# Reordering pairs of VO, weight sums and one residual in the first groups of a gated cross-attention block

## The chip, the cores and the metric

The kernel runs on one core of a Trainium2 chip. The metric is the device time of one execution in microseconds, as the median of several runs. The core has five engines that run side by side, each through its own queue of instructions in order: TensorE (PE in the profile; PEld is its loading of weights), VectorE (DVE), ScalarE (ACT), GpSimd (POOL) and SyncE (SP, which issues most DMAs). They wait for one another by semaphores.

## The reference: what is computed

Four sequences of 2048 rows of 512 features attend to a context of 77 keys with 16 heads of 64, and then go through one linear layer that is chosen from eight; both results are added to x through a gate.

```
x = x + tanh(g_xattn[0]) * xattn(layernorm(x), ctx_768, Wq, Wk, Wv, Wo, bo)
x = x + tanh(g_ffn[0])   * ffn(layernorm(x), W, b, logits, u)

xattn: q = x @ Wq ; k = ctx @ Wk ; v = ctx @ Wv           (16 heads of 64)
       attn = softmax(q k^T / 8) ; out = (attn v) @ Wo + bo
ffn:   idx = argmax(log_softmax(logits) + gumbel(u)) ; out = x @ W[idx] + b[idx]
```

All of it is float32.

## The kernel before, in words

**Folded weights.** The kernel doesn't form q, k and v for all rows. It folds Wq and the keys into one matrix M for each head (`build_m`), and the values and Wo into one matrix VO for each head (`build_vo`, L323). Scores of a group of rows are then x·M, and the attention's output is softmax·VO. VO is made in eight pairs of heads: `build_vo(p, engines)` issues six matmuls (three chunks of rows for each of the two heads, of 64 contracted rows) into six PSUM banks, and six evictions that scale by the gate and go to a staging buffer. The string says which engine evicts: its letters are gone through in turn, "A" is ScalarE (L337), "D" is VectorE (L335). Then four DMAs on SP's queue (L341, L342) store the pair in DRAM (`vo_d`). `load_vo(b)` (L348) loads the part that belongs to sequence b back from DRAM as four blocks into `vo`. There are seven staging buffers; five of them lie in `vo` itself, and go round among heads 2 to 15.

**Groups.** 16 groups of 512 rows are worked on, four to a sequence. Of each group come the scores (`ps_s`), the softmax, the attention's output (`ps_a`), the residual, and the feed-forward (`ps_f`). While group i's softmax runs, TensorE does the attention of group j = i - 1 and then its feed-forward.

**Seven products.** Every large product is done with seven products of half size in place of eight (`Seven`, L441). This needs sums of blocks: four of the weights (`weight_sum`, L119, by GpSimd unless told otherwise) and four of the columns, T1 to T4 (`Columns.sum`, L430, GpSimd). A Seven accumulates in three PSUM regions; `product(s)` (L455) is the matmuls of step s, and `post(s)` (L478) then either copies a region to SBUF on ScalarE (L468, L472: the quarters 11, 22, 12 and last 21), or adds it to a quarter on VectorE (L487). So a later product that accumulates into a region waits for the copy or the addition that reads it: products 2, 4 and 6 of a Seven write the region that post(0), post(2) and post(4) have read. Seven PSUM banks serve all products in turn.

**Softmax of one group.** `s_rows` (L513) transposes scores into rows; `head_max` (L523) takes a quarter's maxima, four quarters ("heads" 0 to 3) to a group; `exps(i, n0, n1)` (L529) issues exponentials n0 to n1 of 64 on ScalarE, 16 to a head; `head_sum` (L538) sums and inverts on VectorE; `head_scale` (L543) scales on GpSimd; `p_columns` (L547) transposes back into `pT` on VectorE, and needs all four heads for each piece.

**Residual.** `residual(j, at, which)` (L556) adds a quarter of the attention's output to x on GpSimd. T1 of the feed-forward's columns (`yc`) is the difference of quarters 12 and 11, so it stands behind the residuals in GpSimd's queue.

**What sets the order.** The order is written out by hand: the order of the calls in the program is the order of each engine's queue. The stretch that the change touches is the start. Ahead of the loop over groups stand pairs 0 to 2 of VO, the scores of group 0, pair 3 (L739, "AAD"), then a loop of six products of group 1's scores (L743) with one pair of VO behind each of the first four products (L755: "DDA", "DDA", "D", "D"), the maxima and exponentials of group 0, and the weight sums of wf (the feed-forward's weight) among them. `e` (L742) says how many exponentials are issued by each step; the rest follow the loop (L764). `load_vo(0)` stands in step 3 (L760). The next loop (L765) does the rest of group 1's scores (`s1`, `s2`, and the last product of `s0`), takes group 0's `p_columns` in steps 1 to 4, and the first three weight sums of vo in steps 3, 4 and 5. Group 1's pass through the loop over groups (i = 1, j = 0) then begins with the attention of group 0 (L866), in whose step 0 the fourth sums of vo and of wf are made (L885, L886); in step 5 come a head's sum, its scaling and the residual of quarter 22 (L906 to L908).

Of the kernel before, what the change touches and what calls it, by code (L numbers as in the profile page):

```python
# [19 lines left out]
def flamingo_block_kernel(  # L20
# [34 lines left out]
    NT, D = x.shape  # L55
# [467 lines left out]
    def head_max(i, h):  # L523
        mx = stat[:, ds((16 + h) * NG, NG)]
        nc.vector.tensor_reduce(mx, head(i, h), AX.X, ALU.max)  # L525
        nmx[h] = small.tile([P, NG], F32, tag=f"nmx{h}", name="nmx")
        nc.vector.tensor_tensor(nmx[h], mx, norms[i].down, ALU.mult)  # L527
# [10 lines left out]
    def head_sum(i, h):  # L538
        sums[h] = sm = small.tile([P, NG], F32, tag=f"sm{h}", name="sm")
        nc.vector.tensor_reduce(sm, head(i, h), AX.X, ALU.add)  # L540
        nc.vector.reciprocal(sm, sm)  # L541
# [195 lines left out]
    s2 = Seven("ps_s", w_scores, xc[1], (4,), SNAP1)  # L737
    head_max(0, 0)
    build_vo(3, "AAD")  # L739
    head_max(0, 1)  # L740
    exps(0, 0, 8)
    e = (8, 16, 24, 32, 41, 50, 57)  # L742
    for s in range(6):  # L743
        s0.product(s)
        s0.post(s)
        if s < 2:
            centre_wf(wfr, 2 * s)
            centre_wf(wfr, 2 * s + 1)
        if s == 2:
            weight_sum(wf, 0)  # L750
            weight_sum(wf, 1)
        if s == 3:
            weight_sum(wf, 2)
        if s < 4:
            build_vo(4 + s, "DDA" if s < 2 else "D")  # L755
        if s < 2:
            head_max(0, 2 + s)
        exps(0, e[s], e[s + 1])
        if s == 3:
            load_vo(0)  # L760
        if 3 <= s:
            head_sum(0, s - 3)
            head_scale(0, s - 3)
    exps(0, 57, 64)  # L764
    for s in range(7):  # L765
        s1.product(s)
        s2.product(s)
        if s == 0:
            s1.post(0)
            s2.post(0)  # L770
            s0.product(6)
            s0.post(6)
            head_sum(0, 3)
            head_scale(0, 3)
        if s == 3:
            norm_step(n1, 2)
        if 1 <= s < 5:
            p_columns(0, (0, 2, 5, 7)[s - 1], (2, 5, 7, 10)[s - 1])
        if s == 2:
            pT[0].sum("T1")  # L780
        if s == 3:
            weight_sum(vo, 0)
        if s == 4:
            weight_sum(vo, 1)
        if s == 5:
            weight_sum(vo, 2)
            for k in range(4):
                s_rows(1, (0, 1, KH, KH + 1)[k], s0.chunk(k // 2, k % 2))
        if 0 < s:
            s1.post(s)  # L790
            s2.post(s)
# [5 lines left out]
    for i in range(1, NGRP):  # L797
        j, f, nx = i - 1, i - 2, i + 1
        n = norms[i]
        last = nx == NGRP  # L800
        swap_m, swap_vo = i % GPB == GPB - 1 and not last, 1 < i and j % GPB == 0
        if 1 < i:

            s0 = scores0(i)
            for s in range(6):
                s0.product(s)
                if s == 0:
                    s0.post(0)
                    if 0 <= f:
                        end_of_ff(f)  # L810
                    p_columns(j, 6, 8)
                    xc[i].sum("T4")
                if s == 1:
                    p_columns(j, 8, 10)
                    if 0 <= f:
                        f_rows(f, ff, 1)
                if s == 2:
                    pT[j].sum("T1")
                    pT[j].sum("T3")
                if 0 < s:  # L820
                    s0.post(s)
                if 0 <= f and s in (2, 3):
                    n.stats(ys[f], 0, 8 * (s - 2), 8)
                if s == 3 and 0 <= f:
                    add_bias(f, nc.gpsimd)
            n.gather()
            for k in range(2):
                s_rows(i, k, s0.chunk(0, k))

            s1 = Seven("ps_s", w_scores, xc[i], (2, 3), SNAP)  # L830
            s2 = Seven("ps_s", w_scores, xc[i], (4,), SNAP1)
            for s in range(7):
                s1.product(s)
                s2.product(s)
                if s == 0:
                    s1.post(0)
                    s2.post(0)
                    s0.product(6)
                    s0.post(6)
                    n.calc()  # L840
                    n.power()
                    for k in range(2):
                        s_rows(i, KH + k, s0.chunk(1, k))
                elif s == 3:
                    n.back()
                if swap_vo and 3 <= s:
                    weight_sum(vo, s - 3, nc.vector if s < 5 else None)
                if 5 <= s and 0 <= f:
                    f_scale(f, n.rs, 5 * (s - 5), 5)
                if 0 < s:  # L850
                    s1.post(s)
                    s2.post(s)
                if s == 5:
                    for k in range(2):
                        s_rows(i, 2 + k, s1.chunk(0, k))
                    s_rows(i, 4, s2.chunk(0, 0))
            for k in range(2):
                s_rows(i, KH + 2 + k, s1.chunk(1, k))
            s_rows(i, KH + 4, s2.chunk(1, 0))
            if swap_m:  # L860
                load_m(nx // GPB)
        if not last:
            norms[nx] = Norms(nx)


        at = Seven("ps_a", w_attend, pT[j], (0, 1), SNAP, bo_c)  # L866
        for s in range(7):
            at.product(s)
            if s == 0:
                pT[j].sum("T2")  # L870
                if 0 <= f:
                    f_scale(f, n.rs, 10, 6)
                    f_add(f, 0, NG, nc.gpsimd)
                    store(f)
                head_max(i, 0)
                head_max(i, 1)
            if s == 1:
                head_max(i, 2)
                head_max(i, 3)
            if 1 <= s:  # L880
                e = (0, 10, 20, 32, 44, 56, 64)
                exps(i, e[s - 1], e[s])
            if s == 0 and i == 1:
                pT[j].sum("T3")
                weight_sum(vo, 3)  # L885
                weight_sum(wf, 3)  # L886
            if s == 2:
                pT[j].sum("T4")
                if swap_m:
                    weight_sum(m, 0)  # L890
                if not last:
                    x_columns(nx)
                    norms[nx].stats(xg[nx], norms[nx].x0, 0, 8)
                head_sum(i, 0)
                head_scale(i, 0)
            if s == 3:
                if not last:
                    norms[nx].stats(xg[nx], norms[nx].x0, 8, 8)
                    if nx + 1 < NGRP:
                        load(nx + 1)  # L900
            if s == 4:
                residual(j, at, "11")
                head_sum(i, 1)
                head_scale(i, 1)
            if s == 5:
                head_sum(i, 2)  # L906
                head_scale(i, 2)
                residual(j, at, "22")  # L908
            if s == 6:
                residual(j, at, "12")  # L910
                residual_last(j, at)
                head_sum(i, 3)
            else:
                at.post(s)
        if j % GPB == GPB - 1:
            load_vo((j + 1) // GPB)
        yc[j] = Columns(xc[j].all, **{f"T{k + 1}": tq[:, k] for k in range(4)})
        yc[j].sum("T1")
        yc[j].sum("T2")
        yc[j].sum("T3")  # L920
        head_scale(i, 3)
        yc[j].sum("T4")


        ff = Seven("ps_f", w_ffn, yc[j], (0, 1), SNAP)
        for s in range(6):
            ff.product(s)
            if s < 2:
                y_rows(j, 2 * s)
            if s == 1 and swap_m:  # L930
                weight_sum(m, 1, nc.vector)
            if not last:
                if s == 1:
                    xc[nx].sum("T1")
                if s == 2:
                    xc[nx].sum("T2")
                if s == 4:
                    if swap_m:
                        weight_sum(m, 2)
                    xc[nx].sum("T3")  # L940
                    if swap_m:
                        weight_sum(m, 3)
            if 2 <= s:
                k = (0, 2, 3, 5, 6)
                p_columns(i, k[s - 2], k[s - 1])
            ff.post(s)
        f_rows(j, ff, 0)


    j, f = NGRP - 1, NGRP - 2  # L950
# [146 lines left out]
```

## Time and profile before

| what | us |
|---|---|
| median of 3 runs | 1249.91 (1249.31 to 1250.05) |
| the profiled execution's own time | 1249.17 |
| its span (first to last instruction) | 1247.1 |
| TensorE busy | 1234.9 (99%) |
| TensorE weight loads busy | 1061.0 (85%) |
| VectorE busy | 908.8 (73%) |
| GpSimd busy | 894.8 (72%) |
| ScalarE busy | 683.6 (55%) |

The span is shorter than the execution's time by what lies before the first and behind the last instruction. All times inside the execution are counted from the first instruction. "Busy" is a share of the whole span; the start, where VO is made, has other limits than the fourteen like passes that follow, so the stretch from 88 to 170 us has to be read by itself, engine by engine. A row in order of time gives the start, the length, the engine, the line, the operation, what it writes and reads, how many instructions are merged in it, and in brackets the idle time before it with what ended that. Where an operation has to wait, the bracket names the engine and tile that it waited for; a matmul's wait shows at its weight load.

### The profile page before, as it was taken

What the parts mean: (1) busy time and instruction counts of PE and PEld (TensorE: products, weight loads), DVE (VectorE), ACT (ScalarE), POOL (GpSimd) and SP (SyncE); (2) the same over time, 40 slices, a digit from 0 to 9 for tenths busy, and PEclk for the clock granted to TensorE, in tenths of its full rate; (3) what the DMA queues carried; (4) which work ended last, traced back from release to release, by engine and by line L of the source; (5) the groups of instructions that cost most, each with busy time, mean ns of one, the idle gap of its engine ahead of it and who ended that gap; (6) DMA issues with size and microseconds to landing.
All of it is one profiled execution on the core that took longest, in us unless ns stands there. A gap on an engine that the chain in (4) does not pass through costs nothing.

```text
span 1247.1 us, 16992 instructions
## 1 busy us (share of the span) xinstructions
PE 1234.9 (99%) x5704; PEld 1061.0 (85%) x5704; DVE 908.8 (73%) x1853; ACT 683.6 (55%) x1957; POOL 894.8 (72%) x484
## 2 busy tenths in 40 slices
PE   9999999999999999999999999999999999999996
PEld 6676888888888888888888888888888888888885
DVE  6778966666977766677776767777776787766577
ACT  4639545638274563827356482745648274554823
POOL 5558885857957785785968778575977877575766
PEclk9999999999999999999999999999999999999999
DMA  9868300314023030304006030202305120010102
GB/s 266 309 194 271 60 1 1 68 43 110 1 51 102 1 68 1 68 22 117 15 1 152 1 68 2 55 14 85 68 1 118 35 62 7 1 34 1 34 1 67
DMA packets 95221, 80.27 MB, mean 64 GB/s; under 512 B 3856, under 2 KB 83088, under 8 KB 95136
## 3 DMA queue, kind: packets, MB, share of 16 engines
q1 hardware_dynamic: 92768, 76.74, 24.2%
q10 hardware_dynamic: 1760, 1.34, 0.4%
q0 software_dynamic: 608, 1.13, 0.2%
q8 instruction: 45, 0.74, 0.2%
q14 instruction: 40, 0.33, 0.1%
HBM read 44.07 MB, written 35.13 MB: 64 GB/s over the span
## 4 chain that ended last, share of the span: by engine, by line
PE 94%; DVE 2%; ACT 1%; DMA 1%; POOL 0%; issue 0%; SPq 0%; DVEq 0%; ACTq 0%; POOLq 0%
PE ps_s L462 37%; PE ps_a L462 36%; PE ps_f L462 15%; PE ps_kv L266 2%; PE ps_vo L332 2%; PE ps_m L296 1%; ACT s L533 1%; DVE s L516 0%; DMA vo<-vo_d 0%; DVE pT L553 0%; PE ps_w L167 0%; DVE t L413 0%; DMA vo_d<-vo 0%; DVE snap L487 0%; POOL xc L559 0%
## 5 line engine op out<-in xcount | busy, mean ns | idle before, releaser
L462 PE MATMUL ps_a<-pT,vo 128*128 128x256 f32 x2240 | 486.2, 379 | 0.0
L462 PEld LDWEIGHTS ps_a<-pT,vo 128*128 128x128 f32 x2240 | 425.6, 190 | 57.9
L533 ACT ACTIVATE s<-s,nmx,up 128x77 f32<-128x77 f32 x1024 | 355.6, 446 | 0.9 <-DVE nmx L527 0.8
L433 POOL TENSOR_TENSOR pT<-pT 128x1280 f32<-128x1280 f32 x64 | 185.8, 2904 | 171.6 <-PE ps_a L462 162.0
L462 PE MATMUL ps_s<-tq,m 128*128 128x256 f32 x1280 | 290.6, 380 | 0.0
L462 PEld LDWEIGHTS ps_s<-tq,m 128*128 128x128 f32 x1280 | 242.6, 190 | 36.2 <-issue 1.6
L468 ACT COPY snap<-ps_s 128x512 f32<-128x512 f32 (+1 forms) x188 | 93.5, 515 | 293.4 <-DVE t L413 131.4
L462 PE MATMUL ps_s<-xc,m 128*128 128x256 f32 x960 | 221.0, 379 | 0.0
L462 PEld LDWEIGHTS ps_s<-xc,m 128*128 128x128 f32 x960 | 182.2, 190 | 27.5 <-DVE vo L335 1.6
L544 POOL TENSOR_TENSOR s<-s,sm 128x1232 f32<-128x1232 f32 x64 | 145.1, 2268 | 48.4 <-DVE sm L541 48.4
L487 DVE TENSOR_TENSOR snap<-snap,ps_s 128x512 f32<-128x512 f32 (+1 forms) x141 | 83.7, 593 | 130.4 <-PE ps_s L462 126.3
L462 PE MATMUL ps_f<-tq,wf 128*128 128x256 f32 x512 | 118.5, 379 | 0.5 <-DVE snap L487 0.4
L553 DVE STREAM_TRANSPOSE pT<-s 128x512 f32<-128x512 f32 x160 | 101.0, 678 | 16.8 <-POOL s L544 16.8
L433 POOL TENSOR_TENSOR tq<-xc,tq 128x512 f32<-128x512 f32 x64 | 85.2, 1332 | 35.1 <-PE ps_f L462 32.6
L394 POOL TENSOR_TENSOR r<-r,neghalf 32x16 f32<-32x16 f32 (+1 forms) x33 | 93.1, 2832 | 22.6 <-DVE r L389 22.0
L462 PEld LDWEIGHTS ps_f<-tq,wf 128*128 128x128 f32 x512 | 97.1, 190 | 14.4 <-issue 0.7
L540 DVE TENSOR_REDUCE sm<-s 128x16 f32<-128x1232 f32 x64 | 91.5, 1430 | 20.7 <-ACT s L533 20.6
L516 DVE STREAM_TRANSPOSE s<-snap 128x512 f32<-128x512 f32 x156 | 99.9, 685 | 6.1 <-ACT snap L468 3.9
L525 DVE TENSOR_REDUCE ps_st<-s 128x16 f32<-128x1232 f32 x64 | 92.4, 1444 | 2.1
L462 PE MATMUL ps_f<-xc,wf 128*128 128x256 f32 x384 | 90.7, 379 | 0.0
L433 POOL TENSOR_TENSOR tq<-xc 128x512 f32<-128x512 f32 x64 | 81.4, 1271 | 6.4 <-DVE xc L408 5.1
L468 ACT COPY snap<-ps_f 128x512 f32<-128x512 f32 x63 | 36.9, 585 | 88.9 <-PE ps_f L462 86.2
(129 smaller groups left out, 1186.1 us busy)
## 6 DMA issues: line engine op xcount, KB each, us to landing
xg<-in_x_dram SPq DMA_DIRECT2D x64, 256.0 KB, 5.9
out_dram<-y SPq DMA_DIRECT2D x60, 256.0 KB, 4.8
vo<-vo_d SPq DMA_DIRECT2D x16, 640.0 KB, 5.6
m<-m_d SPq DMA_DIRECT2D x12, 640.0 KB, 4.1
vo_d<-vo SPq DMA_DIRECT2D x14, 512.0 KB, 3.7
m_d<-vo SPq DMA_DIRECT2D x4, 960.0 KB, 6.1
wq<-in_WqT_dram SPq DMA_DIRECT2D x8, 256.0 KB, 7.0
wq<-in_Wo_dram SPq DMA_DIRECT2D x1, 2048.0 KB, 13.2
```

The costliest lines, as they stand in the source:

```text
L266: nc.tensor.matmul(ps[:, :n], w[:, c, ts(p, P)], keys[:, c].rearrange("p b j -> p (b j)"), start=(c == 0), stop=(c == NCC - 1))
L394: nc.gpsimd.tensor_tensor(r, r, neghalf[:32, : r.shape[1]], ALU.pow)
L433: (engine or nc.gpsimd).tensor_tensor(self.at[name], self.at[a], self.at[b_], op)
L462: nc.tensor.matmul(self.ps[r][:, n, :], self.w(blk, c, pair), self.cols(cname, c), start=(first and n == 0 and c == 0), stop=(c == h - 1), ...
L468: nc.scalar.copy(dst, self.ps[r])
L487: nc.vector.tensor_tensor(c, c, self.ps[r], ALU.add)
L516: nc.vector.transpose(key_chunk(sc[i], k), cols.rearrange("p (g h r) -> p g h r", h=HA, r=R))
L525: nc.vector.tensor_reduce(mx, head(i, h), AX.X, ALU.max)
L533: nc.scalar.activation(head(i, h)[:, g, :], head(i, h)[:, g, :], AF.Exp, scale=norms[i].up[:, g : g + 1], bias=nmx[h][:, g : g + 1])
L540: nc.vector.tensor_reduce(sm, head(i, h), AX.X, ALU.add)
L544: nc.gpsimd.tensor_tensor(head(i, h), head(i, h), sums[h].unsqueeze(2).to_broadcast([P, NG, J]), ALU.mult)
L553: nc.vector.transpose(pT[i].all[:, k, :].rearrange("p (g h r) -> p g h r", h=HA, r=R), key_chunk(sc[i], k))
```

## The change

Six edits, all in the start and in the pass i = 1:

- Pair 4 of VO is built directly behind pair 3, ahead of the loop over group 1's products, with its evictions alternating ("AD"). Pairs 5, 6 and 7 move one step forward in the loop; the strings stay with the step and not with the pair.
- The cuts `e` between the exponentials of group 0 are others.
- `load_vo(0)` moves from step 3 to step 2.
- The fourth weight sum of wf moves from the attention of group 0 to step 3 of the loop over group 1's first products.
- The first weight sum of vo moves from step 3 to step 1 of the next loop, ahead of T1 of `pT`.
- In the pass i = 1 the residual of quarter 22 stands ahead of the third head's scaling on GpSimd. In all later passes it stays behind it.

No operation is added or taken away; three evictions go from VectorE to ScalarE.

```diff
     head_max(0, 0)
     build_vo(3, "AAD")
+    build_vo(4, "AD")
     head_max(0, 1)
     exps(0, 0, 8)
-    e = (8, 16, 24, 32, 41, 50, 57)
+    e = (8, 16, 24, 36, 42, 47, 52)
     for s in range(6):
         s0.product(s)
         s0.post(s)
...
         if s == 3:
             weight_sum(wf, 2)
-        if s < 4:
-            build_vo(4 + s, "DDA" if s < 2 else "D")
+            weight_sum(wf, 3)
+        if s < 3:
+            build_vo(5 + s, "DDA" if s < 2 else "D")
         if s < 2:
             head_max(0, 2 + s)
         exps(0, e[s], e[s + 1])
-        if s == 3:
+        if s == 2:
             load_vo(0)
         if 3 <= s:
             head_sum(0, s - 3)
             head_scale(0, s - 3)
-    exps(0, 57, 64)
+    exps(0, 52, 64)
     for s in range(7):
         s1.product(s)
         s2.product(s)
...
+        if s == 1:
+            weight_sum(vo, 0)
         if s == 2:
             pT[0].sum("T1")
-        if s == 3:
-            weight_sum(vo, 0)
         if s == 4:
             weight_sum(vo, 1)
...
             if s == 0 and i == 1:
                 pT[j].sum("T3")
                 weight_sum(vo, 3)
-                weight_sum(wf, 3)
...
             if s == 5:
                 head_sum(i, 2)
+                if i == 1:
+                    residual(j, at, "22")
                 head_scale(i, 2)
-                residual(j, at, "22")
+                if 1 < i:
+                    residual(j, at, "22")
```

## The prediction

> **What bounds the kernel now.** I read the page first, then the list of who waited for whom on TensorE, then each engine's instructions in order of time from 88 to 170 us, the only stretch that the change touches.
>
> ```profile
> PE 1234.9 (99%) x5704; PEld 1061.0 (85%) x5704; DVE 908.8 (73%) x1853; ACT 683.6 (55%) x1957; POOL 894.8 (72%) x484
> ...
> PE 94%; DVE 2%; ACT 1%; DMA 1%; POOL 0%; issue 0%; SPq 0%; DVEq 0%; ACTq 0%; POOLq 0%
> ```
>
> TensorE is the bound. Its matmuls of 128x256 start every 0.216 us from 125 us to the end of the loop, whatever the other engines do; the 16 us after its last matmul (1231.1 to 1247.1) are not touched. So only two things count: matmul time that goes away, and moments at which a matmul is kept waiting. Of the latter the trace has one in this stretch (below: TensorE's weight loads in order of time, the last column being the idle time before and who ended it).
>
> ```profile
> 165.46 1.70 PEld L462 LDWEIGHTS ps_f<-xc,wf 128*128 128x128 f32 x8
> 167.65 0.94 PEld L462 LDWEIGHTS ps_f<-tq,wf 128*128 128x128 f32 x5 [0.49 <-POOL tq L433]
> ```
>
> The matmul before it starts at 167.18, so this one was due at 167.40 and comes at 167.65: 0.25 us lost, and the next follows after 0.32 in place of 0.216: 0.10 more. It waited for GpSimd's T1 of group 0's feed-forward.
>
> **What is nearly late now.** Each engine's rows in order of time: start, length, engine, line, operation, out<-in, number, idle time before and its releaser. Three rows are of ScalarE (ACT), one of GpSimd (POOL), three of VectorE (DVE):
>
> ```profile
> 90.70 2.55 ACT L337 ACTIVATE vo<-ps_vo,tg 128x512 f32<-128x512 f32 x4 [0.68 <-PE ps_vo L332]
> 93.26 1.28 ACT L533 ACT_TABLE_LOAD   x1
> ...
> 106.48 13.83 ACT L533 ACTIVATE s<-s,nmx,up 128x77 f32<-128x77 f32 x40
> ```
> ```profile
> 116.03 8.94 POOL L544 TENSOR_TENSOR s<-s,sm 128x1232 f32<-128x1232 f32 x4 [4.10 <-DVE sm L541]
> ```
> ```profile
> 120.34 1.44 DVE L540 TENSOR_REDUCE sm<-s 128x16 f32<-128x1232 f32 x1
> ...
> 125.01 4.27 DVE L553 STREAM_TRANSPOSE pT<-s 128x512 f32<-128x512 f32 x7 [2.94 <-POOL s L544]
> ...
> 131.91 0.65 DVE L487 TENSOR_TENSOR sn<-sn,ps_s 128x512 f32<-128x512 f32 x1
> ```
>
> Between 90.70 and 121.5 us ScalarE has no idle time before any instruction above 0.02 us. Its last exponential of group 0 ends at 120.30; VectorE starts the last head's sum 0.04 later, ends the reciprocal at 122.06; GpSimd, busy with the third head, starts the fourth scaling at 122.70 (0.6 us of slack) and ends at 124.97; VectorE transposes at 125.01 and is then without a gap until 146 us. In that stretch its addition of 131.91 ends at 132.56; product 6 of s1 accumulates into the bank that it reads, and loads its weights at 132.65. That is 0.09 us of slack on TensorE.
>
> **The change, part by part.**
>
> 1. *TensorE order.* One block of four score matmuls fewer stands between runs of VO. Blocks behind VO take 1.92 us (92.46 to 94.38) where four matmuls take 4 x 0.432 = 1.73: one return trip less is worth 0.19 us. A pair of VO costs 2.92 either way: the run of three pairs starts them at 49.47, 52.29, 55.22 and ends at 58.14. The Trainium skill's page "TensorEngine Tiling (Array Packing)", section "Tiling Modes", has a rule behind this: a change of tiling mode drains TensorE. By that rule alone the change is a gain; it gives no time.
>
> 2. *Evictions on ScalarE.* The fifth pair (build_vo(4)) had "DDA" (two of six on ScalarE) and has "AD" (three); the sixth keeps DDA; the seventh goes from D to DDA; the eighth stays D. So ScalarE gets 8 + 3 = 11 evictions, VectorE 22 - 3 = 19. The three new ones stand ahead of the table load and of all 64 exponentials. The first run of three pairs shows when they can run: its second pair starts at 52.29 and ScalarE's evictions at
>
> ```profile
> 53.45 0.69 ACT L337 ACTIVATE vo<-ps_vo,tg 128x512 f32<-128x512 f32 x1 [0.38 <-PE ps_vo L332]
> 54.31 0.69 ACT L337 ACTIVATE vo<-ps_vo,tg 128x512 f32<-128x512 f32 x1 [0.17 <-PE ps_vo L332]
> 55.32 0.68 ACT L337 ACTIVATE vo<-ps_vo,tg 64x512 f32<-64x512 f32 x1 [0.32 <-PE ps_vo L332]
> ```
>
> that is 1.16, 2.02 and 3.03 after the pair's start. Here the pair starts at 92.46, so the last eviction runs from 95.49 to 96.17, and the table load starts 0.02 later at 96.19, not 93.26: **ScalarE is 2.93 us late**. Behind it everything is back to back and the number of evictions in the loop is the same (2 + 2), so the last exponential ends at 120.30 + 2.93 = 123.23. The lower end is three evictions without waits, 3 x 0.57 (90.70, 91.28, 91.85) = 1.7; the upper end is in rival B. I take 2.93, the row of the same operation.
>
> 3. *The new cuts of the exponentials* (24, 36, 42, 47, 52). On ScalarE nothing stands between the old cuts behind s = 2, nor between the new ones: the built order of ScalarE differs by the three evictions alone. Nothing, either way.
>
> 4. *VectorE gains 3 x 0.66 (95.55, 96.21) = 2.0 us* before 114 us; the first head's sum starts 1.5 earlier (112.7). It doesn't help: the third and fourth sums wait for exponentials 48 (117.4) and 64 (123.23). Fourth: 123.26 + 1.72 (120.34 to 122.06) = 124.98; GpSimd after 0.13, 2.27 long: 127.38; transposes at 127.42. **VectorE is 2.41 late from there**, and has no gap in which to catch up.
>
> 5. *What TensorE feels.* First, s1's product 2 accumulates into what ScalarE copies after the last exponential (120.19 before, 123.12 now, 0.59 long): due at 122.31, it starts at 123.77. Secondly product 6 of s1: addition ends 132.56 + 2.41 = 134.97, and as at 167.59 to 167.65 the matmul follows 0.06 later: 135.03, against 132.86 before: 2.17, and 0.10 for the restart: 2.27. This contains the first, and swallows the 0.19 of part 1.
>
> 6. *Residual "22" ahead of the scaling* (group 1 alone). Addition 22 is done at 157.9; GpSimd idles 2.72 us before the scaling of 161.52, so the residual (1.26) is free there. The chain to T1 is later by 2.41 (exponentials of group 1 start behind VectorE's maxima, 141.65 + 2.41) and shorter by 1.26: T1 ends at 167.59 + 1.15 = 168.74. The weight load is due at 167.18 + 2.27 = 169.45. So the wait at 167.65 goes: -0.25 - 0.10. Without the residual's move T1 would end at 170.0 and cost 0.6.
>
> 7. *Weight sums.* wf 3 (1.26) goes from 149.00, where GpSimd is busy, to 111.94; GpSimd is idle from there to 116.03 (head sum now 114.4). vo 0 (2.91) goes ahead of pT's T1: it starts at 127.4, after its blocks (landed at 122.13 and 124.56 before; the stores end some 2 us earlier now, as does the load behind them on SP's queue), and ends at 130.3; T1 needs five transposes, 130.5, so it costs nothing. vo 1, vo 2, T2 end at 136.9, 139.8, 142.7; they are needed at 141.9, 146.2, 146.2. The skill's "GPSIMD Engine Reference", section "Specifications", speaks against such overlap: GpSimd's way to SBUF contends with some VectorE instructions. The rows disagree for those here: transposes take 0.67 us with GpSimd idle (126.2) and busy (131.3), a 128x1280 sum 2.91 beside them. If it bit, the 3.5 us to T2's deadline would take it.
>
> **Sum**, against the profiled execution (1249.17 us; span 1247.1 and 2.07 around it): +2.27 - 0.35 = **+1.9**, 1251.1. The profiled one lies 0.74 under the median of the three runs, so on the median: 1249.91 + 1.9 = **1251.8 us**. From the lower end of part 2 (1.7: VectorE 1.2 late) it is +0.7.
>
> **Rivals.**
> - *B, slower by more.* Twelve VO matmuls in a row on seven PSUM banks: VectorE reduces head 0's maximum until 92.51 and frees its banks of pair 3 at 93.18 and 93.82. Going round the seven banks in the order in which they come free, only matmul 4 (due 1.39 behind the pair's start, 93.85) needs one. If an earlier one does, the pair stands still: at worst all six behind 93.82, 1.4 us later, and ScalarE with them: +3.3, 1253.2. It decides from 0.6 us of such waiting on. For it: the built order puts a VectorE wait inside this pair. Against: that matmul is the fourth.
> - *C, hidden.* If group 0's exponentials end no later than some 0.7 us after now, only 0.19 and 0.35 are left: 1249.4; partly hidden, up to 1250.9. For it: ScalarE is busy 55% of the span. Against: not in this stretch.
> - *D, it gains what it moves:* faster by 2.5 us or more. TensorE has no such idle time here.
>
> **How the numbers follow.** 0.2% is 2.5 us, about what a measurement of this kernel can tell from no change. Forecast (1250.9 to 1252.4) 0.63; B 0.20; C 0.15; D 0.02. Faster 0.02; within 0.2% 0.63 + 0.15 = 0.78; slower 0.20. The range runs from inside C to inside B, 1249.8 to 1253.0, which leaves about 2 in 10 out.
>
> **What would show it.** In the profile after: the table load at 96.2; the 64th exponential's end near 123.2; the seven transposes at 127.4; weight loads of ps_s that wait for ScalarE's copy near 123.7 and for VectorE's addition near 135; no wait for tq near 169. If the table load stands at 96 and the transposes still start at 125, steps 4 and 5 are wrong; if product 6 isn't kept, the 0.09 us of slack was misread.

## The result and the profile after

| kernel | median us (lowest to highest) | runs | ratio to the kernel before (95% interval) |
|---|---|---|---|
| before | 1249.56 (1248.51 to 1250.09) | 20 | |
| changed | 1251.54 (1250.59 to 1252.10) | 20 | 1.0017 (1.0011 to 1.0023) |

The changed kernel is 2.0 us slower, by its interval 1.4 to 2.9. The forecast was 1.9, and on the median 1251.8. The profiled execution of the changed kernel took 1252.0 us, its span is 1249.8. First the page:

```profile
PE 1235.7 (99%) x5704; PEld 1061.5 (85%) x5704; DVE 907.2 (73%) x1850; ACT 685.4 (55%) x1960; POOL 895.1 (72%) x484
...
PE 96%; DVE 2%; ACT 1%; POOL 0%; issue 0%; DVEq 0%; POOLq 0%
```

The page hides the case: TensorE is busy 0.8 us more, ScalarE has three instructions more and VectorE three fewer, and the shares are as before. What changed is in the list of who waited for whom on TensorE, here the changed kernel's with all its rows:

```profile
PE ps_w L167 <- DVE tq L163: 1.5, 1, 1.5
PE ps_s L462 <- ACT sn L468: 1.3, 1, 1.3
PE ps_s L462 <- DVE sn L487: 0.7, 1, 0.7
PE ps_f L462 <- DVE snap L487: 0.4, 1, 0.4
```

The first and last were there before (the last is in the tail, at 1234.85 before and 1237.53 now). The two in the middle are new: products 2 and 6 of s1. Short waits are not in this list: the one for T1 at 167.65, which the prediction reads from the weight loads, is missing in that of before. ScalarE in order of time shows where they begin:

```profile
91.47 2.55 ACT L337 ACTIVATE vo<-ps_vo,tg 128x512 f32<-128x512 f32 x4 [0.68 <-PE ps_vo L332]
94.39 0.69 ACT L337 ACTIVATE vo<-ps_vo,tg 128x512 f32<-128x512 f32 x1 [0.38 <-PE ps_vo L332]
95.25 0.69 ACT L337 ACTIVATE vo<-ps_vo,tg 128x512 f32<-128x512 f32 x1 [0.17 <-PE ps_vo L332]
96.25 0.68 ACT L337 ACTIVATE vo<-ps_vo,tg 64x512 f32<-64x512 f32 x1 [0.32 <-PE ps_vo L332]
96.95 1.28 ACT L533 ACT_TABLE_LOAD   x1
...
110.17 13.82 ACT L533 ACTIVATE s<-s,nmx,up 128x77 f32<-128x77 f32 x40
```

Here one correction has to be made before any time is compared. In this execution the first matmul of pair 3 starts at 90.31 us, in that of before at 89.54:

```profile
90.31 5.92 PE L332 MATMUL ps_vo<-wq 64*128 64x512 f32 x24
```

(A pair's six matmuls stand as twelve in the profile, so x24 is two pairs.) Up to there the two programs are the same, so the 0.77 us between are an accident of the execution (over all the kernels below the place varied between 88.8 and 92.8). From here on every time "after pair 3" is counted from that matmul. The table load is 6.65 after pair 3, before 3.72: 2.92 late; the copy of s1 (the row that follows the exponentials) 33.58, before 30.65. From the start of pair 3's first matmul to the start of the kernel's last matmul it takes 1148.81 us, before 1146.90: **1.91 us more**. The same measure serves for all the experiments. It is read from the one profiled execution of each kernel. How far it can be trusted shows behind the products with T1 and T2 of group 0's feed-forward: from the matmul that follows them all ten programs are the same, and from there to the last matmul the ten traces differ by up to 0.08 us.

The new waits, in the weight loads in order of time, and what they wait for on VectorE:

```profile
124.51 2.46 PEld L462 LDWEIGHTS ps_s<-tq,m 128*128 128x128 f32 x12 [1.72 <-ACT sn L468]
...
135.79 2.46 PEld L462 LDWEIGHTS ps_s<-tq,m 128*128 128x128 f32 x12 [1.06 <-DVE sn L487]
...
170.22 1.92 PEld L462 LDWEIGHTS ps_f<-tq,wf 128*128 128x128 f32 x9
```
```profile
124.03 1.44 DVE L540 TENSOR_REDUCE sm<-s 128x16 f32<-128x1232 f32 x1 [3.75 <-ACT s L533]
...
128.19 4.27 DVE L553 STREAM_TRANSPOSE pT<-s 128x512 f32<-128x512 f32 x7 [2.44 <-POOL s L544]
...
135.09 0.65 DVE L487 TENSOR_TENSOR sn<-sn,ps_s 128x512 f32<-128x512 f32 x1
```

VectorE sits idle for 3.75 us until the 64th exponential is done. The seven transposes start at 128.19, less 0.77 of the offset 127.42. The addition ends at 135.74, and product 6's weight load starts 0.05 later. At 170.22 the T1 of the feed-forward is no longer waited for. The first matmul of group 0's attention then starts here, in the kernel before and in the changed one:

```profile
135.45 30.38 PE L462 MATMUL ps_a<-pT,vo 128*128 128x256 f32 x140
```
```profile
138.49 30.38 PE L462 MATMUL ps_a<-pT,vo 128*128 128x256 f32 x140
```

That is 45.91 and 48.18 after pair 3: 2.27 later, which T1's missing wait brings down to 1.91 (the matmul behind the products with T1 and T2 starts 81.67 and 83.58 after pair 3).

### The profile page after: what moved, and what is told of

The parts are those of the page before. It is cut to its first block, busy times and chain, and to the rows that moved or that the text cites. A ratio compares the mean times of both kernels' runs of the same rounds, so it can differ in the third digit from the quotient of the medians.

```text
span 1249.8 us, 16992 instructions
## 1 busy us (share of the span) xinstructions
PE 1235.7 (99%) x5704; PEld 1061.5 (85%) x5704; DVE 907.2 (73%) x1850; ACT 685.4 (55%) x1960; POOL 895.1 (72%) x484
## 4 chain that ended last, share of the span: by engine, by line
PE 96%; DVE 2%; ACT 1%; POOL 0%; issue 0%; DVEq 0%; POOLq 0%
PE ps_a L462 39%; PE ps_s L462 37%; PE ps_f L462 15%; PE ps_kv L266 2%; PE ps_vo L332 2%; PE ps_m L296 1%; ACT s L533 1%; DVE pT L553 0%; PE ps_w L167 0%; DVE t L413 0%; DVE snap L487 0%; POOL s L544 0%; DVE t L1018 0%; DVE y L1022 0%; DVE sm L540 0%
## 5 line engine op out<-in xcount | busy, mean ns | idle before, releaser
L544 POOL TENSOR_TENSOR s<-s,sm 128x1232 f32<-128x1232 f32 x64 | 145.2, 2270 | 49.6 <-DVE sm L541 49.6
```

Source lines behind the costliest of these rows:

```text
L544: nc.gpsimd.tensor_tensor(head(i, h), head(i, h), sums[h].unsqueeze(2).to_broadcast([P, NG, J]), ALU.mult)
```

## Experiments

The theory: ScalarE's lateness of 2.9 us behind pair 3, whatever makes it, goes through the exponentials, the last head's sum and scaling, VectorE's transposes and the addition of s1 to TensorE's product 6. The rivals: TensorE's own order, the banks and stores of the run of two pairs cost; or GpSimd's new order does. Each kernel had 11 timed runs beside 33 of the kernel before (one set of 33 for e1 to e4, another for the rest).

| kernel | median us (before) | ratio (95% interval) | pair 3 to last matmul, us | against before |
|---|---|---|---|---|
| before | | | 1146.90 | |
| changed | | 1.0017 (1.0011 to 1.0023) | 1148.81 | +1.91 |
| e1 | 1250.98 (1249.05) | 1.0015 (1.0006 to 1.0024) | 1148.65 | +1.75 |
| e2 | 1251.17 (1249.05) | 1.0018 (1.0009 to 1.0027) | 1148.90 | +2.00 |
| e3 | 1251.78 (1249.05) | 1.0020 (1.0011 to 1.0029) | 1149.32 | +2.42 |
| e4 | 1251.99 (1249.05) | 1.0021 (1.0012 to 1.0030) | 1149.41 | +2.51 |
| e5 | 1249.26 (1249.43) | 0.9997 (0.9988 to 1.0006) | 1146.59 | -0.31 |
| e7 | 1251.18 (1249.43) | 1.0016 (1.0007 to 1.0025) | 1148.81 | +1.91 |
| e8 | 1248.66 (1249.43) | 0.9996 (0.9987 to 1.0005) | 1146.43 | -0.47 |
| e10 | 1251.47 (1249.43) | 1.0017 (1.0008 to 1.0026) | 1148.83 | +1.93 |

**e4: lateness alone, put into the kernel before.**

```diff
     build_vo(3, "AAD")
+    for _ in range(14):
+        nc.scalar.copy(ez, z)
```

> The kernel before with fourteen copies of a 128x8 tile on ScalarE between pair 3's evictions and the table load (some 2.9 us of work that nothing uses); no instruction of any other engine is moved. Theory: the lateness alone makes the loss: VectorE's transposes start 2.4 us later against the table load's old place, product 6 of s1 waits for the addition, and as the residual isn't moved T1 is late too: +2.3 for product 6, +0.5 at T1 in place of the 0.35 of before, together +2.4 us. Rival (the loss needs the reordered TensorE or SP queue): below +0.7 us.

Measured: +2.51. The fourteen copies on ScalarE:

```profile
93.03 3.15 ACT L741 COPY ez<-z 128x8 f32<-128x8 f32 x14
96.19 1.28 ACT L533 ACT_TABLE_LOAD   x1
```

and TensorE's list:

```profile
PE ps_vo L332 <- ACT vo L337: 1.2, 1, 1.2
PE ps_s L462 <- DVE sn L487: 0.4, 1, 0.4
...
PE ps_f L462 <- POOL tq L433: 0.2, 1, 0.2
```

With the kernel before's own order on the other engines, 3.05 us of lateness (6.77 after pair 3 for 3.72) make the whole loss; the row to set beside it is e3 (+2.42, below), which hasn't the residual's move either. How it is split differs: TensorE stands still earlier, at VO matmuls whose banks ScalarE frees late (1.2 us), in place of product 2. That wait is swallowed: product 6 comes when the addition lets it, whatever was lost ahead of it. The rival that needs the reordered queues falls, as a need. That it could be a second cause was not excluded, as the next run showed.

**e1: pair 4's three evictions taken off ScalarE. The expectation failed.**

```diff
-    build_vo(4, "AD")
+    build_vo(4, "D")
```

> The changed kernel with one string changed: pair 4's six evictions all go to VectorE (D for AD), so ScalarE has its old eight evictions and the rest of the change stands. Theory (the cost is ScalarE's lateness of 2.9 us): the gap between the last eviction of pair 3 and the table load on ScalarE is 0.02 us again, the 64th exponential ends 27.0 us after the table load's start as in the kernel before, no weight load of ps_s waits for ScalarE's copy or for VectorE's addition, and the time is 0.5 us UNDER the kernel before (0.19 for the missing return trip, 0.35 for the T1 wait). Rival (the run of two pairs itself costs: banks, staging buffers, stores): 1.5 to 2 us above the kernel before, with waits of TensorE inside the run.

Measured: +1.75, as if nothing had been removed. The table load is back at its place (3.73 after pair 3, before 3.72), and yet the copy of s1 starts 33.40 after pair 3 (changed 33.58, before 30.65). ScalarE in order of time says where the time went:

```profile
92.56 1.28 ACT L533 ACT_TABLE_LOAD   x1
93.85 2.85 ACT L533 ACTIVATE s<-s,nmx,up 128x77 f32<-128x77 f32 x8
96.71 0.59 ACT L468 COPY snap<-ps_s 128x512 f32<-128x512 f32 x1
98.62 0.69 ACT L337 ACTIVATE vo<-ps_vo,tg 128x512 f32<-128x512 f32 x1 [1.32 <-PE ps_vo L332]
99.72 0.68 ACT L337 ACTIVATE vo<-ps_vo,tg 64x512 f32<-64x512 f32 x1 [0.41 <-PE ps_vo L332]
...
104.74 0.68 ACT L337 ACTIVATE vo<-ps_vo,tg 64x512 f32<-64x512 f32 x1 [0.55 <-PE ps_vo L332]
```

ScalarE now waits for TensorE: 1.32 + 0.41 + 0.55 = 2.28 us of the 2.75 by which the copy is late; the rest lies in rows that no longer overlap the one before them (an eviction takes 0.69 alone and 0.57 in a row), which is not broken down further. The evictions in the loop stand ahead of the next eight exponentials in its queue, and they belong to the pair that TensorE makes in that step. That pair is made later than the pair of the same step was before, as pair 4 was put ahead of it: pair 5 starts 7.77 after pair 3 (88.83 to 96.60), pair 4 started 4.84 after pair 3 (89.54 to 94.38). So there are **two ways to the same lateness**, and cutting one shows the other. The old theory ("the three evictions are the cause") is right for what holds ScalarE in the changed kernel, but not sufficient: the run of two pairs costs by itself. The rival's number came true and its mechanism did not: it wanted waits of TensorE inside the run, and the two pairs take 5.85 there (88.83 to 94.68) for 5.84 in the changed kernel.

**e8 and e10: the second way cut, with and without the first.** In the first two steps of the loop the exponentials go ahead of the pair's evictions, with other cuts, so that ScalarE has work while TensorE makes the pair. e10 has that alone, e8 has `build_vo(4, "D")` as well.

```diff
-    e = (8, 16, 24, 36, 42, 47, 52)
+    e = (8, 18, 28, 36, 42, 47, 52)
...
+        if s < 2:
+            exps(0, e[s], e[s + 1])
         if s < 3:
             build_vo(5 + s, "DDA" if s < 2 else "D")
         if s < 2:
             head_max(0, 2 + s)
-        exps(0, e[s], e[s + 1])
+        else:
+            exps(0, e[s], e[s + 1])
```

> The changed kernel with both ways cut by which ScalarE becomes late: pair 4's evictions all on VectorE (D), and in the first two steps of the loop the exponentials (cuts 18 and 28 for 16 and 24) stand ahead of the pair's evictions in the program, so that ScalarE has work while TensorE makes pairs 5 and 6. New theory (two ways lead to the same lateness: the evictions ahead of the table load, and, if those go, ScalarE's waiting for pairs 5 and 6, which TensorE now makes 2.2 us later; either alone costs 1.8 to 1.9 us): ScalarE has no idle time above 0.1 us from the first eviction of pair 3 to the 64th exponential, its copy of s1 starts 30.6 us after pair 3's first matmul as in the kernel before, TensorE doesn't wait at products 2 and 6 of s1, and from pair 3's first matmul to the last matmul it takes 0.5 us LESS than in the kernel before (1146.4 for 1146.9). Rival (something else in the run of two pairs, as VectorE's six evictions or the stores): +1.5 or more, with VectorE late ahead of 117 us.

> The changed kernel with only the second way cut: the exponentials ahead of pairs 5 and 6's evictions (cuts 18 and 28), pair 4's evictions still AD. New theory: the table load is 2.9 us late as in the changed kernel and nothing catches up: +1.9 us on the kernel before (1148.8 us from pair 3's first matmul to the last), the copy of s1 33.6 us after pair 3's first matmul. Rival (the wait for pairs 5 and 6 was the cause all along): 0.5 us or less above the kernel before.

Measured: e8 -0.47, e10 +1.93; the copy of s1 30.77 and 33.57 after pair 3. With e1 and the changed kernel this makes a square:

| | exponentials behind the pair's evictions | ahead of them |
|---|---|---|
| pair 4 on both engines (AD) | +1.91 (changed) | +1.93 (e10) |
| pair 4 on VectorE (D) | +1.75 (e1) | -0.47 (e8) |

Either way alone holds the loss; both cut, it is gone, and what is left is most of the gain that part 1 and part 6 of the prediction gave (0.19 + 0.35 = 0.54). e10 loses at other places than the changed kernel: like e4 at a VO matmul that waits for ScalarE (0.7 in the list) and at product 6 (0.4). ScalarE in e8:

```profile
93.12 1.28 ACT L533 ACT_TABLE_LOAD   x1
94.42 2.85 ACT L533 ACTIVATE s<-s,nmx,up 128x77 f32<-128x77 f32 x8
...
97.76 3.54 ACT L533 ACTIVATE s<-s,nmx,up 128x77 f32<-128x77 f32 x10
101.19 1.25 ACT L337 ACTIVATE vo<-ps_vo,tg 128x512 f32<-128x512 f32 x2
...
107.83 12.46 ACT L533 ACTIVATE s<-s,nmx,up 128x77 f32<-128x77 f32 x36
```

From the table load to the end of the 36 exponentials no row has an idle time. In TensorE's list both waits for s1 are missing, and the attention starts 45.82 after pair 3 (before 45.91):

```profile
135.22 30.38 PE L462 MATMUL ps_a<-pT,vo 128*128 128x256 f32 x140
```

e8 is faster than the changed kernel (its interval ends at 1.0005, that of the changed kernel begins at 1.0011); against the kernel before the time can't tell it (0.9987 to 1.0005), only the trace can.

**e2: two evictions in place of three, the last at the same place.**

```diff
-    build_vo(4, "AD")
+    build_vo(4, "DDA")
```

> The changed kernel with pair 4's evictions as DDA: two on ScalarE in place of three, the last of them still the pair's sixth. Theory (what counts is when the pair's last eviction is ready, 3.03 us after the pair's start, not how many there are): table load as late as in the changed kernel (within 0.1 us), time +1.9 us on the kernel before. Rival (it is the work of the evictions, some 0.6 us each): a third of the lateness goes, table load 0.6 us earlier, time +1.2 to 1.3 us.

Measured: +2.00, and the table load 6.69 after pair 3 (changed: 6.65).

```profile
94.16 0.69 ACT L337 ACTIVATE vo<-ps_vo,tg 128x512 f32<-128x512 f32 x1 [1.24 <-PE ps_vo L332]
95.20 0.68 ACT L337 ACTIVATE vo<-ps_vo,tg 64x512 f32<-64x512 f32 x1 [0.36 <-PE ps_vo L332]
95.90 1.28 ACT L533 ACT_TABLE_LOAD   x1
```

A third of the work is gone and none of the lateness: the idle time in the brackets grows (1.24 for 0.38). So it is the moment at which the pair's last matmul is done that sets the table load here, and not the work of the evictions ahead of the last. The total can't say this by itself, since the second way would hold the loss anyway; the place of the table load does.

**e3: the residual back behind the scaling**

```diff
-                if i == 1:
-                    residual(j, at, "22")
                 head_scale(i, 2)
-                if 1 < i:
-                    residual(j, at, "22")
+                residual(j, at, "22")
```

**and e5: the residual alone, in the kernel before** (the same edit the other way).

> The changed kernel with the residual of quarter 22 back behind the scaling in the pass i = 1. Theory: T1 ends 1.26 us later, some 0.6 us after its weight load is due, so TensorE waits there again by 0.4 to 0.6 us: +0.5 us on the changed kernel, +2.4 on the kernel before. Rival (T1 has room to spare once TensorE is late): as the changed kernel, +1.9.

> The kernel before with only the residual of quarter 22 moved ahead of the scaling in the pass i = 1. Theory: T1 ends 1.26 us earlier, the one wait of TensorE (0.25 us and 0.10 for the restart) goes: -0.35 us. Rival (GpSimd's order shifts the wait to T2 or T4): no change, with a wait for tq later on.

Measured: e3 +2.42, that is 0.51 over the changed kernel; e5 -0.31. The weight loads of e3, then of e5:

```profile
169.73 1.38 PEld L462 LDWEIGHTS ps_f<-tq,wf 128*128 128x128 f32 x7 [0.64 <-POOL tq L433]
```
```profile
165.31 1.70 PEld L462 LDWEIGHTS ps_f<-xc,wf 128*128 128x128 f32 x8
167.03 2.13 PEld L462 LDWEIGHTS ps_f<-tq,wf 128*128 128x128 f32 x10
```

The move does what it should, in either surrounding, and no wait for tq stands in TensorE's list further on. In e5 the whole gain is there at T1: the matmul behind the products with T1 and T2 starts 81.31 after pair 3, before 81.67, 0.36 earlier; over the whole rest 0.31 is left of that, which the scatter of 0.08 covers. In time alone e5 is within noise (0.9988 to 1.0006).

**e7: the two weight sums of GpSimd back at their old places**

```diff
             weight_sum(wf, 2)
-            weight_sum(wf, 3)
...
-        if s == 1:
-            weight_sum(vo, 0)
...
+        if s == 3:
+            weight_sum(vo, 0)
...
                 weight_sum(vo, 3)
+                weight_sum(wf, 3)
```

> The changed kernel with the two weight sums of GpSimd back at their old places. Theory: they had room there: no wait of TensorE more or less, as the changed kernel within 0.1 us (+1.9 on the kernel before, by the times from pair 3's first matmul). Rival (with VectorE late, wf 3 and vo 0 at their old places make T2 or T4 late): 1 us or more above the changed kernel.

Measured: 1148.81, the changed kernel's own number, and TensorE's list is the changed kernel's line by line. These two edits are worth nothing here. That `load_vo(0)` stands a step earlier has no kernel of its own; in e8, which has it too, no loss is left for it to explain.

## Why the prediction was right, point by point

1. *TensorE order:* 0.19 for a return trip. In the changed kernel two pairs in a row take 5.84 (90.31 to 96.15, where the scores follow), so a pair takes 2.92 there too. Once the pairs are made and before any wait for s1, TensorE is ahead of the kernel before: the run of 20 matmuls of s1 starts 24.09 after pair 3 (114.40), before 24.33 (113.87). That is 0.24: the 0.19, and some 0.05 by which the other runs of VO are shorter. As forecast, product 6 swallows it. e8, where nothing swallows it, keeps 0.09 only: its pair 6 takes 3.17 (102.02 to 105.19) for 3.03 in the changed kernel (102.92 to 105.95), as in e1, which also leaves pair 4 to VectorE. What pair 6 waits for there was not found. So e8's 0.47 is 0.09 for the order, 0.36 for T1 and 0.02 of scatter, where 0.19 + 0.35 were reckoned.
2. *ScalarE 2.93 late:* measured 2.92. The times of readiness taken from the first run of pairs (1.16, 2.02, 3.03 after the pair's start) fit to within 0.02 us (the pair starts 2.92 after pair 3, at 93.23; evictions at 94.39, 95.25, 96.25). The lower end of that step, 1.7 for three evictions back to back, was no bound that could be reached in this order: in e2, with two evictions in place of three, the table load is as late.
3. *The cuts of the exponentials:* the changed kernel's are worth nothing, as said: they changed no order on ScalarE. e8 and e10 show that cuts can count if they move exponentials past an eviction.
4. *VectorE 2.41 late:* transposes at 127.42 forecast, 127.42 measured (128.19 less 0.77).
5. *Product 6 at 135.03:* measured 135.80 less 0.77 = 135.03. Product 2 at 123.77: 124.51 less 0.77 = 123.74. Of the 2.92 VectorE passes on 2.41 and TensorE 2.17. The last 0.24 is more than the 0.09 of slack that the prediction names: that is the weight load's; the matmul itself started 0.30 behind the addition before (132.56 to 132.86) and 0.06 behind it now. The sum used the matmul's, so it isn't touched.
6. *Residual:* the wait for T1 is gone; without the move 0.6 was forecast, e3 measured 0.51. T1 of the feed-forward ends at 169.54 on GpSimd, 168.77 without the offset, where 168.74 was forecast.
7. *Weight sums:* nothing, and nothing (e7). One step on the way was wrong without a price: T2 of `pT` was to end at 142.7, and with the offset taken off ends at about 145.2, as GpSimd waits 2.49 us for TensorE's `ps_a` ahead of it; TensorE has no wait for it in its list. And the rows by which part 7 shows GpSimd and VectorE undisturbed beside each other are of transposes, which read a single tile; they say nothing of VectorE instructions of other kinds.

Two more things were wrong without a price. The prediction took 1231 us as the end of TensorE's last matmul: there the chain that ended last leaves TensorE, but its last eight matmuls start at 1234.85. That tail is the same in both kernels. And the prediction, which reckoned only what was late in the changed order, missed that ScalarE was close to a second wait: with ScalarE in time, it would have waited for pairs 5 and 6, as it does in e1. This moves nothing in the forecast, as the later of the two ways counts. That the way which was missed is the smaller (+1.75 by itself) is luck: nothing in the prediction showed it. It made rival C's condition ("group 0's exponentials end no later") unreachable by the evictions alone, and the expectation for e1 wrong by 2.3 us. Rival B (a matmul of pair 4 that waits for VectorE's bank) didn't occur: the pair ran without a pause.

## What to carry to other kernels

Where one engine is busy 99%, look for the waits that are nearly there: the row that ends 0.09 us ahead of its reader is where a delay of a few microseconds elsewhere comes out, less the slack on the way (here 2.92 us on ScalarE came out as 2.17 on TensorE). An eviction ties its engine to TensorE's position (in e1 ScalarE stood idle for 1.32, 0.41 and 0.55 us ahead of three of them): everything behind it in that engine's queue starts no earlier than the matmul that it reads, so a moved run of matmuls moves the exponentials behind its evictions, even when the evictions themselves are few. And when removing a suspected cause changes nothing, look for a second way to the same moment before dropping the first; only the kernel with both cut tells.

## What the runs showed that was not expected

- The start of pair 3 lies between 88.83 and 90.31 us in nine of the ten profiled executions, whose programs are the same up to there. In the tenth, of e10, it was 92.84, with one wait of TensorE ahead of pair 3 that no other has:

```profile
PE ps_m L296 <- DVE wf L276: 1.9, 1, 1.9
```

  Such an accident is as large as the change. Times counted from a matmul inside the trace agree far better between kernels that should agree: 1148.81, 1148.81 and 1148.83 for the changed kernel, e7 and e10, and 1148.90 for e2.
- Three waits of TensorE cost their length and then 0.10 us for the restart: behind those at 167.65 (before), 124.51 and 135.80 (after) the next matmul follows after 0.32 us in place of 0.216.
